# A four-layer graph network kernel: the attention scores of layers 1 and 3 are made transposed, and norms, masks and memory places change with them

## The chip, the core and the metric

The kernel runs on one core of a Trainium2 chip. A core has several engines that each work through their own queue in order: PE (TensorE, matrix products and transposes into the accumulation memory PSUM), DVE (VectorE), ACT (ScalarE), POOL (GpSimd) and SP (SyncE, which here issues the DMAs). PSUM is used as banks of 128 partitions by 512 float32 numbers. The metric is the time of one execution on the device in microseconds.

## What is computed

The input x holds 32 batches of 512 nodes with 128 features each; adj is one 512 x 512 matrix of zeros and ones for all of them. Everything is float32. Four graph layers follow one another, each as `x = layernorm(x + layer(x))`. The batches don't depend on each other.

- Layer 0: scores `e[i,j] = x[i]·a_i + x[j]·a_j`, normalised over the whole 512 x 512 matrix, multiplied by adj, leaky ReLU (slope 0.2), softmax over i, product with x, sigmoid.
- Layer 1: `h = x Wp + bp`, scores `s_src[i] + s_dst[j]`, leaky ReLU, masked by adj, softmax over j, product with h, layer norm and ReLU (gives h_gat); then `(1+eps) h_gat + A h_gat`, a matrix W1, layer norm, ReLU, a matrix W2, and ReLU of the sum with h_gat.
- Layer 2: two matrices, mixed by a constant 512 x 512 attention matrix that depends on adj only.
- Layer 3: as the first half of layer 1, with other weights and with self loops in the mask; softmax, product with h, then ELU.

The core of layers 1 and 3 is, in the reference's words:

```python
e = leaky_relu(e_src[:, :, None] + e_dst[:, None, :], 0.2)
e = where(adj == 0, -1e9, e)
attn = softmax(e, axis=-1)
h_prime = einsum('bij,bjo->bio', attn, h)
```

## The kernel before

A batch is held as four tiles of 128 nodes (NB = 4), a 512 x 512 score matrix as four tiles of 128 x 512. The setup (`prepare_l1`, `prepare_l2`, `prepare_l3`, lines 598 to 771) makes the masks, the transposed matrices and the constants once. Then each batch goes through `statistics0` (line 889), `layer0` (956), `layer1` (981), `layer2` (1042) and `layer3` (1067).

The functions don't emit instructions at once. A recorder (`Recorder`, line 281) writes down every operation with what it reads and writes, for all 32 batches; every operation is emitted at line 432, which is why the profile shows that one line. `Recorder.order` (line 349) then replays an order kept in the text `ORDER`: each byte chooses one of the operations whose inputs are ready. On the way it gives every tile a place: SBUF buffers (BUFFERS = 70), small buffers (SMALLS = 110), PSUM banks (BANKS = 8). In gaps that its own cost list foresees on PE it puts filler transposes, named warm (`fill`, line 395). Each engine then runs its queue strictly in this order, with some ten batches in flight at a time.

The parts that the change touches, by tile name as the profile prints it:

- Layer 0: DVE forms `e_r = (p_s_r + tb) * adj_t` out of PSUM, ACT applies Prelu and then Exp with a sum.
- Layers 1 and 3 (`masked_softmax`, line 863): the row of s_dst is spread over all partitions, by four transposes into PSUM (p_d_g, p_d_a) or, for layer 3 of batches 5 to 29, by DMA through a line in memory (turnedd_a, lined_a, d_a). DVE adds the mask to it and takes each row's maximum in one instruction (`e_g`, `e_a`); ACT applies Prelu (with s_src as bias) and Exp (with the maximum as bias, and a sum read out). Rows i lie on the partitions.
- The product with h needs j on the partitions, so PE transposes each e in 16 blocks (p_t_g, p_t_a); DVE copies them out times adj (nm_g), or ACT copies them out (nm_a).
- Layer 1's first norm: mean and variance of p_o_g by DVE (st_go, mv_go), two passes over hg_g by DVE, ReLU by ACT. Its second norm: the same statistics on zz_g, then a scaling by DVE.
- `layer_norm` (line 809): statistics by DVE, the power -0.5 by POOL (rs_r, rs_g, rs_t, rs_a), the scaling by ACT with two pointers (x_r, x_g, x_t, x_a).
- Layer 3's end: Relu, Exp and a third step on ex_a by ACT, then DVE.

POOL has the powers, three 128 x 512 products a batch (xs_r, hb_g, xbias_t) and set-up work.

Of the kernel before, what the change touches and what calls it, by code (L numbers as in the profile page):

```python
# [17 lines left out]
P = 128  # L18
# [3 lines left out]
FILL = -3.0e38  # L22
# [3 lines left out]
BANKS = 8  # L26
FIRST = 5
FINAL = 6
# [3 lines left out]
ROWS_FROM = 5  # L32
ROWS_LATE = 2
SMALLS = 110
BUFFERS = 70
LINES = 12

ORDER = """
c-mchiH;jFlpNW-@0;vPnz45`2?FH*e=kJ`2!co&*)x*5$;WziutkMgA8{P7cnIh0WXEw3A^uYck<_oahyTIt&yV`CSO0u|pZ8aM&L$~+I2BZ}H?K;cp
Iaa2(Vm0SgR0|s=s_sCQd;L}(@I@55?gI5HmwKgEw@-(iZ!y3Lp!P;ZPYT>=%Wn30&UB+v|6Ke%^a_TjBEY9R$YJB$mcYxmZfH!wM|7v4)woUC-tEIZ^
<T>|Cxyoqzd!DoDYUr@4fTZTWy20-UV-+<yKlRtTe_+!?n>u38fX+(i&qqH=GM$1y@oS?S1eG2k^#g=d9Mo`m9Yh+Td1<mNDz7T+GTTXN7UvNsEJOEtL
++;BJ+*7B4GdwZtoG|IhPWYS1o<fI;pNDvp1(%gQ^eqA@z}UxkxZXkV?6x)>XE(3)$ja~48!mxRmGNm-=Uhf+~u1%*;FNXdj_LSt@%av~TbhvHafE+jj
cRmZ^&jb9If;c&_1AqBN~ho!_t=V<aySbI3jgrwF}WvP&d6^!DOR5R{{FesFxj-a|yaKag3ha@-^<%%fhq|;V%fl{Ix_&8Ub?E2y`7%3*Ay^h-LDRCz;
RxTY@AO^)n5P>JBlMYd%PFMr4g>_gH)Z4k>Ja@_(hxKF<pOuzN&ruVO0|$c&V%2t$a9HE_5-Z`b3K&{Agr|6`vUoG!L&2n^IB-~EQY(p|n2hOksH#+oi
a5tB@zGaQraD5%zg0`_AdwJM4DCZmriUlgQBCzh544FuuLvd%#!(iAx(nuxjWev4l+t;c<Kaj&k*Z+S;k9wp6vqj17!TkgH_S*te-fscKkRN)cPN_vEr
aBE;)+tw0aC2qUMwI0%iuIQOvFqQx}!QO(4>xHq%;z02%`kAV<wgxe>lKEL?KH^T>H+O8<iKHt<2nnphMGMb%`#KrZRqbNf{B87EHGo^t^GoM3b^R4jc
{V2-czy)-uC1#dr^D4sj48G)>&0792=o4h69~pwc;3U5Y47kI4s9g7BjpwXuMM9W;=`=V)9wf@X|LmxU=2OJEGQ1f!77F$WI9A|HlGK=5z^B?9glI^0P  # L50
v3DuG)!YqlF?*^q<MQQOdDmdB?C^CStIFv>SHNY+XuBMrc=m9h;gXKiA383!KTIgj#G{s8FgaNB869DBs3CSy<HH5<(=W%jHaXcVYZ-jwcB=C*_af~J4
fni}LQV@?$;ojn5sWpt}6g){fhmu5)0>o3S5;epEUJ4i;Pa%lSY9OU(G&oM%u1qx=0A13D0p_v>oOLjRrC{1Klo03w1|@(_k{~G_$t;txL{SqObI&Fv3
miumLd+ZM+1n$8unTSo$V%xLZHykBp&i4Yuo%pvmX3LF>!I+3uBWKq6cGgmA#veZVi7FrqgE_ZubIl6I-?|YN(iq257Y)LVbOx1CSn0DVx5-WChuvXz&
iL1izy5N+mm3D17q534TL}tXNoXY0F5z7fD5Pw6&R0-L?^KTHD;d^m@~SPv52S~-|s=Y9uZZ~&Dd-XG>_>Xo#}RY>0xWLsT8iK)<swEixP!sPXrmD6$g
@oS{P?Hryeno=ugpmZ&<{Vn@FNUTzeZsQ>Che+_K8OJ6xdF5gshV>J{Y}Hv*_eV>)e;#+m@o5G)a5NTGyaMT|Kr1?+m6e3UpXmPaQLMUp`s4!|%@m^~<
z#(*ZV*Z{myL>r|D1s=C#gHRwTQfHP@U|7MxY~WR-TzugnK?k5f#wKex!_u(=p~$E$@GY806FPrFt;*(x-9k7x797gpp=&Y(NUT@cJ5`631(R?kf@3To
wKaA{kd6)zIi<Z7`#?|>6MY7hGEdr8E(6ZTqejm_4mhw3LeIdTVtYA7b*!+IDQ(hFwiST^jtMR9i!I=k%Kr&4=uCnnJqqLj<QOuSHE^g%2pOR1w#C6pG
2<v@r8H4v7e*chRwd+?dd-E9m{QCc{)HN_H?bKYlu0Y;=bRb7$Jx*?zg#$DSR;lW(g+zJ#;-Y!8CP^8L0xwzzz_9YYqcfSQfR8Qnjl05sqq4#9JbHc?A
Ck;QRflujwU?IN%<KggRn4{_eepUAcW{k!tAQA0_v2#MBheGM*wobAtRVo0L*XBPf20bS#nxs$Rsl`<zh^j8~j<oWTvi7%GUA#-vpfkrXI51M>n7`A2F
qxQcDgjRW!!nbTh4@mU>*VT#3KA_qUb#?*>(Y*XxVpQyk~x34B=?PKO?b!9Y(ZDRGA6B?&NE4mK-T4+l|gl|5J)K`O3bQi>UiWsVG9f<ymA*3?4Ym<BF  # L60
_S45(7dV;obR4r53h2e_NA$mtcY=NSZTOtT)(8!=k4v9II;d?9$WKQ=AVc;HRRQQ;KBa2a?NSUOxwVa{-VC#}pMwUtnZVIGXt5nJ!=8(sc;jk9OA(R;j
# [59 lines left out]
class Ring:  # L121


    def __init__(self, pool, shape, bufs, name, psum=False):
        self.pool, self.shape, self.name, self.psum = pool, shape, name, psum
        self.slots = [Slot(self, i) for i in range(bufs)]
# [104 lines left out]
def cost(engine, op, args, k):  # L231
# [5 lines left out]
    if engine == "pe":  # L237
        if op == "transpose":
            return 110, 180
        n = args[2].n  # L240
        return (860, 180) if n > 256 else (225, 180)
# [913 lines left out]
```

## Time and profile before

| | |
|---|---|
| median of 3 runs | 1021.2 us (1021.13 to 1022.13) |
| span of the profiled execution | 1019.8 us |
| its time outside the span | not shown by the page; the median is 1.4 us above the span |
| PE, DVE, ACT, POOL busy | 998.3, 968.0, 961.9, 406.4 us |
| most costly groups | products p_o_a, p_o_r, p_o_g: 141.1, 136.2 and 129.2 us of PE |

The span is what passes from the first to the last instruction. "Busy" is the time in which an engine had at least one instruction running, set-up instructions not counted. An instruction's mean duration is longer than its share of the engine when the next one starts before it has ended; the timeline, which lists starts, shows the share.

### The profile page before, as it was taken

How to read it: one execution, taken by the hardware profiler on the slowest of the kernel's cores; microseconds unless marked ns; L12 is line 12 of the kernel's file. 1: busy time of each engine (PE TensorE's matmuls, PEld its weight loads, DVE VectorE, ACT ScalarE, POOL GpSimd, SP SyncE). 2: the span in 40 equal slices, each digit the busy share in tenths (PEclk: the TensorE clock that was granted, in tenths of full speed). 3: DMA queues.
4: the chain of work that ended last, by engine and by line, in shares of the span. 5: the costliest groups of instructions: out<-in, count | busy, mean ns of one | idle time of the engine just before them, and what ended most of it. 6: DMA issues, size and time to landing. Idle time of an engine off the chain costs nothing.

```text
span 1019.8 us, 22710 instructions
## 1 busy us (share of the span) xinstructions
PE 998.3 (98%) x7281; PEld 853.5 (84%) x7281; DVE 968.0 (95%) x4378; ACT 961.9 (94%) x2297; POOL 406.4 (40%) x510
## 2 busy tenths in 40 slices
PE   8999999999999999999999999999999999999994
PEld 7778789879889888888888897888888888779994
DVE  7899999999899999999999999999999998998997
ACT  3597899999999999999999999999999999999997
POOL 7534432352324425343343515342452435244242
PEclk9999999999999999999999999999999999999998
DMA  7000000000110110100111011001001000001003
GB/s 185 28 2 1 1 2 1 2 1 1 32 33 1 36 40 2 42 18 27 33 32 33 22 37 38 22 1 53 12 29 36 11 12 22 23 11 33 12 22 103
DMA packets 42599, 26.81 MB, mean 26 GB/s; under 512 B 4336, under 2 KB 38768, under 8 KB 42480
## 3 DMA queue, kind: packets, MB, share of 16 engines
q1 hardware_dynamic: 42192, 24.84, 8.8%
q8 instruction: 58, 0.95, 0.4%
q14 instruction: 61, 0.50, 0.2%
q10 hardware_dynamic: 288, 0.52, 0.1%
HBM read 16.91 MB, written 8.44 MB: 25 GB/s over the span
## 4 chain that ended last, share of the span: by engine, by line
DVE 39%; ACT 31%; PE 23%; POOL 3%; issue 2%; DMA 1%; POOLq 0%; SPq 0%; DVEq 0%; ACTq 0%
ACT e_a L432 7%; ACT e_g L432 5%; ACT e_r L432 4%; DVE e_g L432 4%; PE p_o_r L432 4%; DVE e_r L432 4%; DVE nm_g L432 3%; PE p_g_g L432 3%; ACT ex_a L432 3%; PE p_o_g L432 3%; DVE e_a L432 3%; DVE zz_g L432 3%; DVE hg_g L432 3%; ACT x_g L432 2%; DVE xa_r L432 2%
## 5 line engine op out<-in xcount | busy, mean ns | idle before, releaser
L432 PE MATMUL p_o_a<-h_a,nm_a 128*128 128x128 f32 x1024 | 141.1, 275 | 0.3 <-ACT nm_a L432 0.3
L432 PE MATMUL p_o_r<-xs_r,e_r 128*128 128x128 f32 x1024 | 136.2, 275 | 0.4 <-POOL xs_r L432 0.3
L432 PEld LDWEIGHTS p_o_a<-h_a,nm_a 128*128 128x128 f32 x1024 | 128.4, 192 | 5.8 <-issue 5.3
L432 PEld LDWEIGHTS p_o_r<-xs_r,e_r 128*128 128x128 f32 x1024 | 125.6, 192 | 4.4 <-issue 3.3
L432 PE MATMUL p_o_g<-h_g,nm_g 128*128 128x128 f32 x1024 | 129.2, 275 | 0.0
L432 PEld LDWEIGHTS p_o_g<-h_g,nm_g 128*128 128x128 f32 x1024 | 122.5, 192 | 4.9 <-issue 4.1
L432 PE MATMUL p_y_t<-l_rest_t,x_g 128*128 128x512 f32 x256 | 120.9, 593 | 0.2 <-ACT x_g L432 0.2
L432 PE MATMUL p_g_g<-a1t,hg_g 128*128 128x512 f32 x256 | 118.7, 595 | 0.7 <-ACT hg_g L432 0.6
L432 ACT ACTIVATE e_a<-e_a,nmx_a 128x512 f32<-128x512 f32 x128 | 92.7, 739 | 2.5 <-DVE nmx_a L432 2.5
L432 ACT ACTIVATE e_r<-e_r,r_r 128x512 f32<-128x512 f32 x128 | 92.6, 728 | 0.4
L432 ACT ACTIVATE e_g<-e_g,nmx_g 128x512 f32<-128x512 f32 x128 | 91.6, 727 | 1.2 <-DVE sh_r L432 0.8
L432 DVE SCALAR_TENSOR_TENSOR e_r<-p_s_r,tb_r,adj_t 128x512 f32<-128x512 f32 x128 | 92.0, 746 | 0.5 <-PE p_s_r L432 0.5
L432 ACT ACTIVATE e_a<-e_a,sd_a 128x512 f32<-128x512 f32 x128 | 89.8, 740 | 0.0
L432 ACT ACTIVATE e_g<-e_g,sd_g 128x512 f32<-128x512 f32 x128 | 86.7, 730 | 0.6 <-DVE mx_g L432 0.3
L432 DVE TENSOR_TENSOR nm_g<-p_t_g,adj_t 128x512 f32<-128x512 f32 x128 | 82.9, 684 | 0.9 <-PE p_t_g L432 0.8
L432 PE MATMUL p_t_a<-ident,e_a 128*128 128x128 f32 x512 | 82.2, 273 | 0.8 <-ACT e_a L432 0.7
L432 DVE CUSTOM_DVE_ANT_0 e_g<-p_d_g,mask 128x512 f32<-128x512 f32 x128 | 82.2, 688 | 0.6 <-PE p_d_g L432 0.5
L432 ACT ACTIVATE e_r<-e_r 128x512 f32<-128x512 f32 x128 | 77.8, 636 | 5.0 <-DVE e_r L432 4.6
L432 PEld LDWEIGHTS p_g_g<-a1t,hg_g 128*128 128x128 f32 x256 | 44.7, 190 | 39.4 <-issue 35.3
L432 PE MATMUL p_t_g<-ident,e_g 128*128 128x128 f32 x512 | 73.0, 273 | 0.2 <-DVE sh_r L432 0.2
L432 POOL TENSOR_TENSOR hb_g<-hg_g,b_bc 128x512 f32<-128x512 f32 x32 | 41.7, 1303 | 68.2 <-ACT hg_g L432 67.9
L432 PEld LDWEIGHTS p_y_t<-l_rest_t,x_g 128*128 128x128 f32 x256 | 43.6, 191 | 30.1 <-issue 27.3
(211 smaller groups left out, 2902.3 us busy)
## 6 DMA issues: line engine op xcount, KB each, us to landing
x_in<-in_x SPq DMA_DIRECT2D x32, 256.0 KB
out<-x_a SPq DMA_DIRECT2D x32, 256.0 KB
d_a<-lined_a SPq DMA_DIRECT2D x25, 256.0 KB
lined_a<-turnedd_a SPq DMA_DIRECT2D x100, 0.5 KB
adj_n<-in_adj ACTq DMA_DIRECT2D x2, 256.0 KB
adj_n<-in_adj SPq DMA_DIRECT2D x2, 256.0 KB
w<-in_L_gnn_W SPq DMA_DIRECT2D x3, 64.0 KB
a_ij<-in_L_gnn_a SPq DMA_DIRECT2D x1, 128.0 KB
```

The lines of the kernel that those rows point to most:

```text
L432: f(*[real(a) for a in args], **{n: real(a) for n, a in k.items()})
```

## The change

Leaky ReLU can be written as `0.2 t + 0.8 max(t, 0)`, and with `t = s[i] + d[j]` the part `0.2 s[i]` cancels in the softmax over j, so that `exp(0.8 (max(d[j], -s[i]) - top[i]) + 0.2 d[j])` is left, where top[i] is the row's maximum of d with the mask, times 1.25 (and the mask with it). This is computed with j on the partitions from the start:

- `score_rows` takes the row maximum (top) as before, from p_d_g or p_d_a, into a PSUM corner and without using the tile that it writes; makes `bend` on DVE, spreads it over the partitions by four transposes (p_g_g, p_g_a), and spreads top by DMA (turnedm, linem, m_g, m_a) for every batch of both layers.
- Layer 1: DVE forms `max(p_g_g, d[j]) - m_g` in a PSUM bank (p_e_g), ACT applies Exp in place, DVE multiplies by adj_t (nm_g). Layer 3: DVE forms `max(p_g_a, d[j]) + mask3_t` (e_a), POOL subtracts m_a, ACT applies Exp. The transposes of e, nm_a and both Prelus are gone.
- h gets a 129th column that gives the row sums out of the product (`products`); ACT writes h_g with a bias instead of DVE. Products have 129 columns, features 131. The weights are centred over features at set-up, so that means vanish.
- Layer 1's norms: ACT squares with a sum instead of DVE's statistics; hg_g by a product with gat_g in PSUM and one pass with max; the second scaling by ACT (zs_g).
- x_g and x_t are scaled without being shifted (`scaled`); x_r and x_a keep the shift.
- Layer 0: ACT applies Prelu out of PSUM with tb as bias, POOL multiplies by adj_t, ACT applies Exp.
- Layer 3's end: one Exp by ACT, a product and minimum by POOL, then DVE in PSUM.
- One PSUM bank ("own") is taken out of the ring for operands of DVE: a_ij, top, some statistics. BANKS = 7, BUFFERS = 57, eight buffers of their own for h, SMALLS = 120.
- A new ORDER text; some entries of the cost list differ.

The diff, cut to its core (set-up, cost list and the order text left out):

```diff
-BANKS = 8
+BANKS = 7
-BUFFERS = 70
+BUFFERS = 57
+FEATS = 8
...
+    feats = Ring(big, [P, NB * HW], FEATS, "feat")
+    own = V(Tl(Ring(ps, [P, 512], 1, "own", True, True), "own"))
...
+    a_ij = own[:, 0 : 2 * D].rearrange("p (k d) -> p k d", k=2)
+    R.dve.tensor_copy(a_ij, a_both)
...
+    def scaled(dst, y, r):
+        for c in range(NB):
+            R.act.activation(dst[:, c, :], y[:, c, :], AF.Identity, scale=r[:, c : c + 1])
+    def normalised(dst, y, more, name, b, by_act=True):
+        mv = corner([P, NB, 2], "mv" + name, b)
+        statistics(y, mv)
+        ve = small([P, NB], "ve" + name)
+        R.dve.tensor_scalar(ve, mv[:, :, 1], LN_EPS, None, ALU.add)
+        r = power(ve, name)
+        mr = corner([P, NB], "mr" + name, b)
+        R.dve.tensor_tensor(mr, mv[:, :, 0], r, ALU.mult)
+        shift = small([P, NB], "sh" + name)
+        R.dve.tensor_scalar(shift, mr, -1.0, more, ALU.mult, ALU.add)
...
+    def features(xt, wx, more, name):
+        h = V(Tl(feats, "h" + name)).rearrange("p (c d) -> p c d", c=NB)
+        for k in range(0, NB, 2):
+            p = bank("h" + name)[:, 0 : 2 * HW].rearrange("p (c d) -> p c d", c=2)
+            for c in range(2):
+                R.pe.matmul(p[:, c, :], xt[:, blk(k + c)], wx, start=True, stop=True)
+            R.act.activation(h[:, k : k + 2, :], p, AF.Copy, bias=more)
+        return h
...
+    def score_rows(h, mask, name, b):
+        pd = rows_of(h[:, :, DST], "d" + name)
+        top = corner([P, NB], "top" + name, b)
+        for c in range(NB):
+            R.dve.tensor_tensor_reduce(
+                buffer("any" + name), pd, mask[:, c, :], 1.25, LOWEST, ALU.add, ALU.max, top[:, c : c + 1]
+            )
+        bend = small([P, NB], "bend" + name)
+        R.dve.scalar_tensor_tensor(bend, top, 0.8, h[:, :, SRC], ALU.mult, ALU.min)
+        top_row = rows_by_dma(top, "m" + name)
+        low = small([P, NB], "low" + name)
+        R.act.activation(low, h[:, :, DST], AF.Copy, scale=LEAKY)
+        return rows_of(bend, "g" + name), top_row, low
...
     def layer0(xb, s, r, tb, b):
-            R.dve.scalar_tensor_tensor(t, p_s, tb[:, j : j + 1], adj_t[:, j, :], ALU.add, ALU.mult)
-            R.act.activation(t, t, AF.Prelu, alpha=LEAKY)
+            if by_pool(b, j):
+                R.act.activation(t, p_s, AF.Prelu, bias=tb[:, j : j + 1], alpha=LEAKY)
+                R.pool.tensor_tensor(t, t, adj_t[:, j, :], ALU.mult)
...
     def layer1(xb, b):
+        h = features(xt, C["l1_wx"], 0.0, "_g")
+        pg, top, low = score_rows(h, C["mask1"], "_g", b)
-        e, z = masked_softmax(sd, C["mask1"], "_g", False)
         for j in range(NB):
-            pt = bank("t_g")
-            for c in range(NB):
-                R.pe.transpose(pt[:, blk(c)], e[c][:, blk(j)], ident)
-            R.dve.tensor_tensor(nm[j], pt, adj_t[:, j, :], ALU.mult)
+            e = bank("e_g")
+            R.dve.scalar_tensor_tensor(e, pg, h[:, j, DST : DST + 1], top, ALU.max, ALU.subtract)
+            R.act.activation(e, e, AF.Exp, bias=low[:, j : j + 1], scale=0.8)
+            R.dve.scalar_tensor_tensor(nm[j], e, 1.0, adj_t[:, j, :], ALU.min, ALU.mult)
+        po = products(nm, h, "_g")
...
+                R.act.activation(
+                    buffer("any_go")[:, 0:D], p[:, c, 0:D], AF.Square, accum_out=sq[:, 2 * k + c : 2 * k + c + 1]
+                )
...
+            R.dve.tensor_tensor(
+                p[:, :, 0:D], p[:, :, 0:D], C["gat_g"].unsqueeze(1).to_broadcast([P, 2, D]), ALU.mult
+            )
+                R.dve.scalar_tensor_tensor(
+                    hg[:, 2 * k + c, :], p[:, c, 0:D], r[:, 2 * k + c : 2 * k + c + 1], C["gat_nb"], ALU.mult, ALU.max
+                )
...
+            R.act.activation(buffer("any_gz")[:, 0:D], zz[:, c, :], AF.Square, accum_out=sq[:, c : c + 1])
+        scaled(zs, zz, power(ve, "_gz"))
...
     def layer3(xb, b):
+        for j in range(NB):
+            R.dve.scalar_tensor_tensor(
+                e[j], pg, h[:, j, DST : DST + 1], C["mask3_t"][:, j, :], ALU.max, ALU.add
+            )
+            R.pool.tensor_tensor(e[j], e[j], top, ALU.subtract)
+            R.act.activation(e[j], e[j], AF.Exp, bias=low[:, j : j + 1], scale=0.8)
+        po = products(e, h, "_a")
...
+            R.act.activation(ex[:, c, :], po[c // 2][:, c % 2, 0:D], AF.Exp, scale=rz[:, c : c + 1])
+        R.pool.tensor_scalar(ex, ex, math.exp(-1.0), 1.0, ALU.mult, ALU.min)
```

## The prediction

> **What bounds the kernel now.** First the page's first two parts and the windows: is one engine short of time, or are they all?
>
> ```profile
> PE 998.3 (98%) x7281; PEld 853.5 (84%) x7281; DVE 968.0 (95%) x4378; ACT 961.9 (94%) x2297; POOL 406.4 (40%) x510
> POOL 7534432352324425343343515342452435244242
> PEclk9999999999999999999999999999999999999998
> ...
> 500.00:600.00 100.00, 99.54 (x749) 86.72 (x748) 99.18 (x453) 100.00 (x242) 36.69 (x46) 1.00 0.09 25
> 1000.00:1020.00 20.00, 6.93 (x58) 6.28 (x56) 12.75 (x59) 12.95 (x37) 6.35 (x10) 0.81 0.42 119
> ```
>
> PE, DVE and ACT are all full; only POOL has room. The granted clock is full. The chain that ended last confirms it: it hops over all three, and no line of code carries more than 7%.
>
> ```profile
> DVE 39%; ACT 31%; PE 23%; POOL 3%; issue 2%; DMA 1%; POOLq 0%; SPq 0%; DVEq 0%; ACTq 0%
> ```
>
> So the forecast is a sum for each engine, and the largest decides. A busy PE may hide gaps, so next the timeline: does the next matmul start where the last one's share ends?
>
> ```profile
> 209.91 0.60 PE L432 MATMUL p_t_a<-ident,x_t 128*128 128x128 f32 x4
> 210.34 1.88 PE L432 MATMUL p_y_t<-l_rest_t,x_g 128*128 128x512 f32 x4
> 212.06 0.38 PE L432 MATMUL p_o_r<-xs_r,e_r 128*128 128x128 f32 x2
> ...
> 250.40 3.73 PE L432 MATMUL p_o_g<-h_g,nm_g 128*128 128x128 f32 x32
> 253.97 1.88 PE L432 MATMUL p_y_t<-l_rest_t,x_g 128*128 128x512 f32 x4
> ```
>
> From start to start (a matmul is two records, a transpose one): a 128-column matmul 3.57/16 = 0.223 us, a 512-column one 1.72/2 = 0.86, a transpose 0.43/4 = 0.11. Counted out: 2387 x 0.223 + 288 x 0.86 + 1983 x 0.11 = 998, the busy time of the page. PE is packed; its 21.5 us of idle lie at the ends (12.2 after the last matmul, 1.5 at the start, 2.9 in one wait).
>
> For DVE and ACT I take pitches too, start to start in the timeline of 300 to 700, since an instruction's mean overlaps its successor. DVE: 128x512 with a pointer 0.655 (e_r), without 0.60 (nm_g), maximum 0.61, 128x128 with pointer 0.26, 128x256 0.34, statistics 0.195 + 0.08, four-column steps 0.07. ACT: 128x512 with a pointer 0.61, Prelu without 0.52, copy from PSUM 0.47, sum read-out 0.10; 128x128 with two pointers from SBUF 0.39, with one from PSUM 0.25.
>
> **The change part by part.** Counts are from the instruction order of both programs; 32 batches.
>
> PE. The 1024 transposes of e_g and e_a go. New are the rows of bend (256 transposes) and 100 more of p_d_a, which came by DMA; 16 for mask3_t; 58 fewer warm fillers: -710 x 0.11 = -78.1. Five or six small set-up matmuls: +1.3. Products of 129 columns instead of 128, features of 131 instead of 130: p_h_a x4 (two matmuls of 130) takes 0.45, so at most +2.3. Sum 998.3 - 74.5 = 924.
>
> DVE, per batch. Gone: e_r 4 x 0.655; nm_g from p_t_g 4 x 0.60; zz scaling 4 x 0.29; the second pass over hg 4 x 0.26; h_g 2 x 0.34; the statistics of o_g and z_g 8 x 0.275; small steps (sd, nmx, ve_go, two shifts, tb) and late copies 1.4: together 11.5. New: p_e_g 4 x 0.655; nm_g from p_e_g 4 x 0.60; e_a 4 x 0.655; the gat_g product 2 x 0.34; small steps (bend, mr, ve, the second dev, halves of y_a, turned, reciprocals) 0.75: together 9.1. Net -2.4 x 32 = -77, +4 of set-up (weight means, a_ij to PSUM, b1): 895.
>
> ACT, per batch. Two of three Prelus go (4 x 0.61 each) and the third now has a pointer (+0.2); the sums of e_g and e_a 8 x 0.10; nm_a copies 1.7; the whole-tile steps on ex_a and hg_g's Relu 1.5; x_g and x_t lose the bias pointer, 8 x 0.1. New: squares of o_g and z_g 8 x 0.25, scaling of z_g 4 x 0.25, h_g 0.5, squares of the sum column and low 0.5. Net about -5.5 x 32 = -176, +5 set-up: 791.
>
> POOL. Two more 128x512 products in every j: 256 of them. Nearest rows:
>
> ```profile
> L432 POOL TENSOR_TENSOR hb_g<-hg_g,b_bc 128x512 f32<-128x512 f32 x32 | 41.7, 1303 | 68.2 <-ACT hg_g L432 67.9
> L432 POOL TENSOR_TENSOR xs_r<-x_in,rz_r 128x512 f32<-128x512 f32 x32 | 33.7, 1053 | 57.6 <-DVE rz_r L432 23.7 <-issue 7.8 <-PE p_o_t L432 6.2
> ```
>
> 256 x 1.30 = 333 (1.05 would give 269; I take hb_g, which reads two full tiles as the new ones do). With ex_a 18, ve_go 9, tb 9, less ve_r and ve_a 17: about 758. POOL stays under PE, with some 20% left. What waits on it: xs_r, five powers a batch and xbias queue behind the products, so each may come one or two products (1.3 to 2.6 us) later; 11 batches are in flight in both orders (products of layer 0 ahead of those of layer 3), so I cost this at nothing in the middle.
>
> [...]
>
> Does a fuller POOL stall DVE? The trace shows when it does:
>
> ```profile
> 506.37 1.17 DVE L432 TENSOR_SCALAR zz_g<-zz_g,mv_gz,rs_gz 128x128 f32<-128x128 f32 x1
> 506.41 1.04 POOL L432 TENSOR_TENSOR xs_r<-x_in,rz_r 128x512 f32<-128x512 f32 x1 [2.50 <-DVE var_r L432]
> ```
>
> 0.33 us of work took 1.17 until POOL's product was done: all operands in SBUF. The maximum over p_d_g (one operand in PSUM) takes 0.690 alone and 0.687 beside POOL. In the new program every large DVE step has a PSUM operand or is a statistic (st_a: 0.282 and 0.275), but for the last three batches' x_a; so I add nothing.
>
> DVE writing to PSUM has no row: 12 large and some 20 small such writes a batch. Reading PSUM costs DVE nothing (y_t from p_o_t 685 ns, y_a from SBUF 684). The largest effect of place in the trace is ACT's, 0.05 us (a whole tile takes 0.47 when read from PSUM by xt_g's copy, 0.52 when read from SBUF by hg_g's Relu). So per write between -0.05 and +0.05: DVE 895 - 51 to 895 + 51. I take 0, DVE's own row, and keep both ends. [...]
>
> DMA and SP. Every layer 1 and 3 now gets its maximum by DMA: 64 rows instead of 25.
>
> ```profile
> 453.85 2.07 SPq L432 DMA_DIRECT2D lined_a<-turnedd_a  x4
> 457.08 0.33 SPq L432 DMA_DIRECT2D d_a<-lined_a  x1
> ```
>
> SP is held 3.6 us a row, 230 us in all with the wait for the line, and the row is there at most 7.4 us after turning (3.6, and the first 256 KB of adj_n landed within 3.83). Behind such a wait on SP stand x_in and out, both early or free in the middle. 39 more broadcasts of 256 KB are 10 MB on queues that are under 10% busy. Layer 3 waits for its row on POOL, whose other products queue behind; layer 1 on DVE at p_e_g, and a late row there stops all batches' DVE steps, then ACT and PE. While 11 batches are in flight 7 us are covered: nothing; in the last ones the cover is gone.
>
> Ends. Before the first p_o_r POOL now has four products more, 5.2 us, and PE has set-up matmuls to fill them with: between 0 and 5, I take +2. At the end POOL has 20 products (26 us) for the last five batches while PE needs 80 x 0.223 = 18 us for their products, and the rows' 7 us: between 0 and 10, I take +4. The steps after the last matmul are the same in number (12 us).
>
> Sum: 924 + 21.5 + 2 + 4 = 951.5 of span. Around the span lie 1.4 us (median 1021.2 less 1019.8; the page has no time of the profiled execution itself): **953 us**, -6.7%.
>
> **The rivals.** *DVE becomes the bound*, by writes to PSUM or by steps that wait in its order for POOL (nm_g for the Exp, hg_g for rs_go, y_a for ex_a). For: 895 is only 29 under PE, and in the old kernel DVE had 52 us of idle with PE as its bound. Against: PSUM reads are free. At 0.05 us a write DVE has 946, and with the old ends 967 to 1000.
>
> *PSUM banks run out: slower.* There are 7 instead of 8 for tiles, and a tile stays longer: e_g (DVE, ACT, DVE) 2.1 us x 4, o_g through squares, power and hg_g 7.4 x 2, o_a 5.5 x 2, z_g 6.3; all tiles of a batch sum to about 91 us by pitches (before: 58). 91 x 32 / 7 = 416 us at least. It decides once holding stretches to 1020/416 = 2.45 times these. In the old trace p_d_g is held 3.84 us (median) where pitches give 3.1, p_h_g 2.26 where they give 1.07: 1.2 to 2.1 times. At 2.6 the span would be 1082. For it: short tiles stretch most. Against: most of the sum is in long ones.
>
> *Little gain because the removed work was beside other work*: can't be all, since all three full engines lose 74 to 180 us; if POOL's queue or the row's latency costs PE 1.5 us a batch, 1000.
>
> **How the numbers follow.** PE stays the bound: 0.66, 941 to 965 (924 plus 16 of ends that can't go, to 924 plus 41). DVE or waits: 0.22, 965 to 1000. Between 1000 and the old time: 0.04. Slower by banks: 0.07; unchanged 0.01. 0.2% is what a measurement tells here. Faster 0.92. 940 to 995 leaves out some 0.03 below and 0.15 above (0.03 of the DVE case, and all beyond 1000).
>
> **What would show it.** Right: p_t_g and p_t_a from e gone, PE busy near 924 and 99 of 100 us in the middle windows, DVE near 895, ACT near 790, POOL near 760; POOL products at 1.3 us; DVE's p_e_g at e_r's 746 ns. Wrong: PE with gaps in the middle, released by nm_g or e_a (DVE or POOL late) or by a reader of a PSUM tile (banks); DVE writes to PSUM longer than rows that write SBUF; POOL over 90%.

## The result and the profile after

The changed kernel takes 1063.8 us (median of 4 runs, 1063.6 to 1064.6), the kernel before 1021.2 in the same session: 1.0418 times as long, 95% interval 1.0403 to 1.0433. It is slower by 4.2%; the forecast was 953 us, 6.7% faster. The profiled execution has a span of 1062.9 us.

First the busy times of the page of the changed kernel, and its slices for the granted clock:

```profile
PE 965.6 (91%) x6583; PEld 794.6 (75%) x6583; DVE 954.7 (90%) x3635; ACT 816.0 (77%) x2399; POOL 770.0 (72%) x819
...
PEclk9989999999999999999999999999999999999996
```

The work moved as the change says: PE has 698 instructions fewer, ACT lost 146 us, POOL gained 364. That POOL's 770.0 is near the 758 of the forecast is luck: ex_a alone came to 42 us more than was put down, other rows to some 30 less. But DVE has 954.7 where I expected 895, and no engine is full: a program with four engines at 91, 90, 77 and 72% waits for itself. The clock is granted but for the ends.

The stretches of the same two programs show where. Columns are the window, its length, the busy time of PE, PEld, DVE, ACT and POOL, then the granted clock, the DMA share and GB/s. Kernel before, first 100 us and last 120:

```profile
0.00:100.00 100.00, 94.25 (x655) 80.02 (x656) 88.06 (x348) 68.01 (x151) 51.92 (x69) 0.98 0.22 55
900.00:1019.80 119.80, 106.93 (x824) 94.90 (x823) 105.50 (x456) 112.84 (x289) 43.59 (x61) 0.97 0.13 39
```

Changed kernel, the same ends, and the window from 500 to 600 that the prediction showed:

```profile
0.00:100.00 100.00, 80.22 (x600) 74.79 (x601) 83.00 (x435) 78.20 (x188) 82.40 (x107) 0.93 0.28 71
500.00:600.00 100.00, 93.90 (x631) 74.67 (x630) 95.51 (x377) 79.25 (x241) 74.88 (x79) 1.00 0.14 41
943.00:1062.90 119.90, 92.86 (x624) 77.81 (x622) 98.27 (x372) 74.44 (x212) 89.11 (x82) 0.90 0.14 38
```

PE lost 14 us of work in the first 100 and 14 in the last 120, and in the middle it is no longer full; DVE is the fullest there. The timeline of PE has holes that the old one hadn't; here one of 1.05 us, which DVE's y_a ended:

```profile
412.49 1.05 PE L434 MATMUL p_o_r<-xs_r,e_r 128*128 128x128 f32 x8
414.59 0.71 PE L434 MATMUL p_h_a<-l_wx,xt_a 128*128 128x131 f32 x4 [1.05 <-DVE y_a L434]
```

What is dear is in the groups (busy time and mean of one, then idle time before them; an aggregate is the step that makes a mean and a variance out of six numbers). POOL and DVE of the changed kernel:

```profile
L434 POOL TENSOR_TENSOR e_a<-e_a,m_a 128x512 f32<-128x512 f32 x128 | 161.4, 1279 | 18.7 <-DVE e_a L434 9.4 <-DMA m_a<-linem_a 7.2 <-DVE rz_a L434 1.0
L434 POOL TENSOR_SCALAR ex_a<-ex_a 128x512 f32<-128x512 f32 x32 | 61.8, 1933 | 12.5 <-ACT ex_a L434 10.8
...
L434 DVE BATCH_NORM_AGGREGATE own<-st 128x2 f32<-128x6 f32 x256 | 47.3, 185 | 5.4
L434 DVE DVE_READ_ACCUMULATOR2_ANT own<- 128x1 f32 x256 | 36.3, 142 | 0.0
L434 DVE DVE_READ_ACCUMULATOR2_ANT n_r<- 128x1 f32 x216 | 17.9, 83 | 0.0
L434 DVE BATCH_NORM_AGGREGATE mv_g<-st 128x2 f32<-128x6 f32 x128 | 14.6, 159 | 0.0
```

Two rows of the kernel before stand against them, POOL's step on ex_a (a multiply and an add there, in the three batches where POOL had it) and the read-out of a maximum into SBUF:

```profile
L432 POOL TENSOR_SCALAR ex_a<-ex_a 128x512 f32<-128x512 f32 x3 | 1.9, 621 | 3.3 <-ACT ex_a L432 3.3
...
L432 DVE DVE_READ_ACCUMULATOR2_ANT mx_g<- 128x1 f32 x128 | 11.4, 89 | 0.0
```

Two things stand out. POOL's step on ex_a takes 1933 ns; I had put 18 us for the 29 that are new, which is 0.62 each, the price of the old row. And the same DVE steps are longer where they write the PSUM tile own than where they write SBUF (n_r, mv_g, the old mx_g): the read-out of a sum 142 against 83 and 89 ns. From start to start the difference is larger, in DVE's timeline of the changed kernel:

```profile
403.56 0.30 DVE L434 BATCH_NORM_AGGREGATE mv_t<-st 128x2 f32<-128x6 f32 x3
403.78 0.45 DVE L434 BATCH_NORM_STATS2 st<-y_r 128x6 f32<-128x128 f32 x2
404.15 0.85 DVE L434 BATCH_NORM_AGGREGATE own<-st 128x2 f32<-128x6 f32 x4
404.90 0.15 DVE L434 BATCH_NORM_AGGREGATE mv_g<-st 128x2 f32<-128x6 f32 x1
...
405.61 0.68 DVE L434 CUSTOM_DVE_ANT_0 any_g<-p_d_g,mask 128x512 f32<-128x512 f32 x1
406.21 0.14 DVE L434 DVE_READ_ACCUMULATOR2_ANT own<- 128x1 f32 x1
406.39 0.69 DVE L434 CUSTOM_DVE_ANT_0 any_g<-p_d_g,mask 128x512 f32<-128x512 f32 x1
```

Four aggregates into own take 0.75 us (404.15 to 404.90), 0.19 each; three into mv_t take 0.22, 0.07 each. A maximum with its read-out takes 0.78, where the kernel before had 0.61. And the largest wait of DVE is for POOL's slow step:

```profile
DVE p_o_a L434 <- POOL ex_a L434: 32.9, 28, 2.5
```

The theory after this look: two prices were wrong, ex_a on POOL and small writes to PSUM on DVE, and DVE became the bound. The rivals: waiting in POOL's queue, PSUM banks, the order text itself.

### The profile page after: what moved, and what is told of

Read it like the earlier page. It is cut to its first block, busy times and chain, and to the rows that moved or that the text cites. A ratio compares the mean times of both kernels' runs of the same rounds, so it can differ in the third digit from the quotient of the medians.

```text
span 1062.9 us, 21689 instructions
## 1 busy us (share of the span) xinstructions
PE 965.6 (91%) x6583; PEld 794.6 (75%) x6583; DVE 954.7 (90%) x3635; ACT 816.0 (77%) x2399; POOL 770.0 (72%) x819
## 5 line engine op out<-in xcount | busy, mean ns | idle before, releaser
L434 POOL TENSOR_TENSOR e_a<-e_a,m_a 128x512 f32<-128x512 f32 x128 | 161.4, 1279 | 18.7 <-DVE e_a L434 9.4
L434 POOL TENSOR_TENSOR e_r<-e_r,adj_t 128x512 f32<-128x512 f32 x128 | 160.6, 1278 | 14.1 <-ACT e_r L434 13.6
L434 PE MATMUL p_o_a<-h_a,e_a 128*128 128x129 f32 x1024 | 138.1, 282 | 10.5 <-ACT e_a L434 8.8
L434 PEld LDWEIGHTS p_o_a<-h_a,e_a 128*128 128x128 f32 x1024 | 128.4, 197 | 17.2 <-ACT e_a L434 10.3
L434 PE MATMUL p_o_g<-h_g,nm_g 128*128 128x129 f32 x1024 | 130.3, 276 | 4.5 <-DVE y_a L434 2.1
L434 ACT ACTIVATE e_a<-e_a,low_a 128x512 f32<-128x512 f32 x128 | 91.9, 735 | 26.3 <-POOL e_a L434 25.8
L434 DVE CUSTOM_DVE_ANT_0 any_g<-p_d_g,mask 128x512 f32<-128x512 f32 x128 | 88.2, 689 | 6.4 <-PE p_d_g L434 2.4
L434 DVE SCALAR_TENSOR_TENSOR p_e_g<-p_g_g,h_g,m_g 128x512 f32<-128x512 f32 x128 | 93.6, 749 | 0.2
L434 DVE CUSTOM_DVE_ANT_0 any_a<-p_d_a,mask 128x512 f32<-128x512 f32 x128 | 88.0, 687 | 5.9 <-PE p_d_a L434 1.8
L434 DVE SCALAR_TENSOR_TENSOR e_a<-p_g_a,h_a,mask_t 128x512 f32<-128x512 f32 x128 | 90.5, 740 | 1.8 <-PE p_g_a L434 1.8
L434 POOL TENSOR_SCALAR ex_a<-ex_a 128x512 f32<-128x512 f32 x32 | 61.8, 1933 | 12.5 <-ACT ex_a L434 10.8
```

What stands on the lines that cost most here:

```text
L434: f(*[real(a) for a in args], **{n: real(a) for n, a in k.items()})
```

## Experiments

### The prices by themselves

A kernel of its own runs each step in rows of equal instructions: first seven forms on POOL, 128x512 each (lines 40 to 52), then small and large steps on DVE (66 to 86).

```python
pool.tensor_scalar(g, a, 0.5, 1.0, ALU.mult, ALU.add)    # 40, 8 times
pool.tensor_scalar(g, a, 0.5, 1.0, ALU.mult, ALU.min)    # 42
pool.tensor_scalar(g, a, 1.0, None, ALU.min)             # 44
pool.tensor_scalar(g, a, 0.5, None, ALU.mult)            # 46
pool.tensor_tensor(g, a, b, ALU.mult)                    # 48
pool.tensor_scalar(g, a, 0.5, 0.1, ALU.mult, ALU.max)    # 50
pool.tensor_scalar(g, a, 0.5, 1.0, ALU.add, ALU.mult)    # 52
```

> A kernel of its own that computes nothing of the reference: it runs each disputed step alone, in rows of equal instructions, POOL first and then DVE, so that neither disturbs the other. Theory 1 (prices of two new forms were missed): POOL's 128x512 tensor_scalar takes about 1.9 us whenever a minimum or maximum is one of its operations and 0.62 us for multiply and add; DVE's aggregate of six numbers takes 0.08 us from start to start when it writes SBUF and 0.19 when it writes PSUM, a four-column product 0.07 and 0.14 to 0.18, the sum read-out of a maximum about 0 and 0.12 more; 128x512 steps that write PSUM or SBUF take the same 0.60 to 0.66. Theory 2 (the slowness in the changed kernel comes from other work beside it, such as shared tiles, POOL's or DVE's neighbours): alone, ex_a's form takes 0.62 and the small steps take the same 0.07 to 0.09 into PSUM as into SBUF.

Groups of POOL:

```profile
L42 POOL TENSOR_SCALAR g<-a 128x512 f32<-128x512 f32 x8 | 15.3, 1918 | 0.6
L50 POOL TENSOR_SCALAR g<-a 128x512 f32<-128x512 f32 x8 | 15.3, 1918 | 0.6
L46 POOL TENSOR_SCALAR g<-a 128x512 f32<-128x512 f32 x8 | 11.9, 1488 | 0.6
L44 POOL TENSOR_SCALAR g<-a 128x512 f32<-128x512 f32 x8 | 11.9, 1485 | 0.6
L48 POOL TENSOR_TENSOR g<-a,b 128x512 f32<-128x512 f32 x8 | 10.1, 1262 | 0.5
L52 POOL TENSOR_SCALAR g<-a 128x512 f32<-128x512 f32 x8 | 4.9, 618 | 0.6
L40 POOL TENSOR_SCALAR g<-a 128x512 f32<-128x512 f32 x8 | 4.9, 617 | 4.0 <-DMA a<-in_x 3.4
```

Timeline of DVE, whole rows of the small steps (24 aggregates into SBUF, 24 into PSUM; 16 products of four columns into SBUF, 16 into PSUM, 16 that read PSUM):

```profile
84.36 1.69 DVE L66 BATCH_NORM_AGGREGATE s<-st 128x2 f32<-128x6 f32 x24
85.96 5.33 DVE L68 BATCH_NORM_AGGREGATE p<-st 128x2 f32<-128x6 f32 x24
91.20 1.22 DVE L71 TENSOR_TENSOR s<-s,first 128x4 f32<-128x4 f32 x16
92.34 3.25 DVE L73 TENSOR_TENSOR p<-s,first 128x4 f32<-128x4 f32 x16
95.49 1.19 DVE L75 TENSOR_TENSOR s<-p,first 128x4 f32<-128x4 f32 x16
```

Theory 1 holds for POOL, the aggregates and the products, with nothing beside the steps. With a minimum or a maximum as second operation a step takes three times one that multiplies and adds (1918 ns against 617); what I hadn't expected is that one operation alone (1485 for a minimum, 1488 for a multiplication) is dearer than a multiply-and-add. An aggregate takes 0.067 us from start to start into SBUF and 0.218 into PSUM, a four-column product 0.071 and 0.197; reading PSUM costs nothing (0.068). The large step takes the same into either (8 in 6.25 and in 6.31 us, 0.78 each, which is more than the 0.66 at most that the theory gave; why was not looked for). The sum read-out is not settled by this run: a maximum with its read-out took 0.73 us from start to start into SBUF and 0.79 into PSUM, a difference of 0.06 and not 0.12.

So for these small steps the price of PSUM lies on the destination (0.13 to 0.15 us more) and not on the source (0.068 us from PSUM, 0.071 from SBUF).

### The two prices in the kernel: one, the other, both

```diff
-        R.pool.tensor_scalar(ex, ex, math.exp(-1.0), 1.0, ALU.mult, ALU.min)
+        R.pool.tensor_scalar(ex, ex, math.exp(-1.0), 0.0, ALU.mult, ALU.add)
```

> The changed kernel with one operation of one POOL step altered: ex_a is multiplied by exp(-1) and gets 0 added, in place of the minimum with 1 (so positive values of the last layer are wrong); order, tiles and waits are the same. Theory 1 (ex_a is three times dearer than I put it, and DVE stands behind it in its queue): the step takes 0.62 us, POOL's sum falls by 42 us to about 728, the 33 us that DVE waits for it at p_o_a shrink to under 10, and the time falls by 15 to 35 us, to 1029 to 1049. Rival (DVE has its bound elsewhere and the wait only moves): DVE waits as long for the next late step, and the time falls by less than 8 us.

This kernel leaves the minimum out, so its time is that of less than the whole computation. Measured: 1034.5 us (1.0127 of the kernel before, 1.0110 to 1.0144), 29.3 less than the changed kernel. ex_a took 618 ns, POOL 727.1, and the wait shrank:

```profile
DVE p_o_a L434 <- POOL ex_a L434: 3.6, 6, 1.2
```

Theory 1, in its range: what went is 29.3 us of the 32.9 that DVE had waited; its own sum all but stayed (951.0). Idle time of DVE is time of the kernel here.

Then the small results, in one SBUF tile instead of the PSUM tile:

```diff
+    nook = V(Tl(Ring(big, [P, 256], 1, "nook", True, True), "nook"))
...
-        t = own[:, at : at + n]
+        t = nook[:, at - 2 * D : at - 2 * D + n]
```

> The changed kernel with all the small corners that it keeps in the PSUM tile own (means and variances of two norms, mr, top, and the deviations of layer 0) put into one SBUF tile instead, shared in the same way, with the same order; a_ij stays in PSUM. Theory 1 (small DVE writes to PSUM cost some 0.1 us more each): the aggregates fall from 0.19 to 0.08 us from start to start, DVE's sum falls from 955 to about 890, and since DVE is 95% busy in the middle the time falls by 35 to 60 us, to 1004 to 1029. Theory 2 (the shared tile's waits of DVE on itself are the cost, not the place): the aggregates stay near 0.19, DVE near 955, and the time within 10 us of 1064. Theory 3 (the place in PSUM is what keeps these steps from waiting for POOL): the four-column steps now wait for POOL's products, up to 1.3 us at each of some 6 a batch, and the time rises by 20 us or more.

Measured: 1044.5 us (1.0238, 1.0222 to 1.0253), 19.3 less, and DVE's sum fell by 5 only. The time lies outside all three ranges; theories 1 and 3 are both at work. Start to start, with idle times left out, the 256 read-outs went from about 30 us to under 1 and the 256 aggregates of own from about 45 to 20: some 54 us gained. It is not the read-out's own place alone: the one of dev_r writes SBUF in both programs, and it took 142 ns where the step in front of it wrote eight columns to PSUM and 80 ns here. But steps that now have all tensors in SBUF wait for POOL's products, as a later run with less work on POOL shows (bend_g 437 to 251 ns). Groups of DVE:

```profile
L434 DVE SCALAR_TENSOR_TENSOR bend_a<-nook,h_a 128x4 f32<-128x4 f32 x32 | 15.4, 483 | 0.0
L434 DVE SCALAR_TENSOR_TENSOR bend_g<-nook,h_g 128x4 f32<-128x4 f32 x32 | 14.3, 448 | 0.0
L434 DVE TENSOR_TENSOR nook<-nook,rs_r 128x4 f32<-128x4 f32 x32 | 11.0, 343 | 1.0 <-POOL rs_r L434 1.0
L434 DVE TENSOR_SCALAR sh_r<-nook 128x4 f32<-128x4 f32 x32 | 10.4, 324 | 0.2
```

In the changed kernel these take 143 to 164 ns. The difference in these four rows and the seven like them (ve, dev, sq, sh_a, mr_a) is 55 us. Theory 2, that the shared tile is at fault, falls: the tile is as shared as before and its aggregates take 0.08.

> Both edits together: the minimum left out of ex_a (so positive values of the last layer are wrong) and the small corners in SBUF. Theory 1 (two mis-sized prices are most of the miss): DVE 890, POOL 728, and the time between 965 and 1000, of which up to 25 us are the slower start and the tail. Rival (the order and POOL's queue cost PE as much by themselves): still 1020 or more, with PE idle for waits on POOL and DVE steps that move from one row to the next.

Both edits: 1013.1 us (0.9925, 0.9904 to 0.9946), 50.7 less; the single gains add up to 48.6. That is above the range that theory 1 gave, since DVE's sum stayed at 946 with those waits in it. The short pauses between DVE's instructions (under 0.25 us) fell from 24.9 us in the changed kernel to 4.7, which the busy times don't show.

### An operand in PSUM, but which

> The changed kernel with both prices mended and nothing left out: mv, mr and top lie in an SBUF tile; the four-column steps that read them (bend, ve, mr, shift) take their constant (0.8, 1e-5, 1, -1) as a pointer to a column in PSUM, so that one operand stays there; ex_a becomes 1 - relu(1 - ex/e), a whole-tile Relu on ACT and a multiply-and-add on POOL in place of the minimum. Order as in the changed kernel. Theory 1 (an operand in PSUM, be it only the pointer, keeps a step from waiting for POOL): bend, ve, mr and shift go back to 0.15 us each, DVE's sum falls from 946 in the run with both edits to about 900, and the time from 1013 to between 975 and 1000. Rival (a pointer doesn't count as the operand): these steps stay at 0.25 to 0.48 us, DVE stays near 945 and the time at 1005 to 1020.

```diff
-        R.dve.scalar_tensor_tensor(bend, top, 0.8, h[:, :, SRC], ALU.mult, ALU.min)
+        R.dve.scalar_tensor_tensor(bend, top, c08, h[:, :, SRC], ALU.mult, ALU.min)   # c08: a column in PSUM
```

Measured: 1041.4 us (1.0213, 1.0174 to 1.0252). The rival: a pointer doesn't count. DVE's sum is 960.7, above the 946 of both edits: the rows of bend, ve, mr and shift grew from 84 us to 100. The time is above the rival's range as well; in this version DVE waits 17.1 us for ex_a, behind ACT's Relu and POOL's step. Groups of DVE:

```profile
L434 DVE SCALAR_TENSOR_TENSOR bend_g<-nook,own,h_g 128x4 f32<-128x4 f32 x32 | 15.9, 497 | 0.1
L434 DVE SCALAR_TENSOR_TENSOR bend_a<-nook,own,h_a 128x4 f32<-128x4 f32 x32 | 14.0, 440 | 0.0
```

An output in PSUM doesn't count either, as a later run shows, in which mr reads two SBUF tiles and writes own:

```profile
L434 DVE TENSOR_TENSOR own<-nook,rs_r 128x4 f32<-128x4 f32 x32 | 11.3, 354 | 4.3 <-POOL rs_r L434 3.1
```

That run is the next, with the means alone in SBUF and ex_a without POOL:

> The changed kernel with nothing left out and the same order, mended by what the runs so far taught. Means and variances (mv) of two norms go to SBUF, so the 256 aggregates should take 0.07 us from start to start in place of 0.19 (-30 us of DVE); top, mr and the deviations stay in PSUM, so bend, mr and shift keep an operand there and don't wait for POOL. ve is added on POOL just before the power (64 x 0.3 = 19 us of POOL, -5 of DVE). ex_a is made on ACT alone as Exp(-Relu(1 - p rz)), with the negated rz copied by ACT, and has no POOL step (POOL -62, ACT about +25). Theory (DVE's sum is the bound, and the time is that sum plus some 66 us of start, tail and single waits, as in the three runs without the wait for ex_a: 1013 against 946, 993 against 926, 1039 against 973): DVE about 918, the time 975 to 995, faster than the kernel before. Rival (the wait for ex_a and POOL's place in the chain give way to waits for ACT, which gets the work): DVE near 920 but p_o_a waits 20 us or more for ACT's ex_a, and the time is 1000 to 1025.

```diff
-        R.dve.tensor_scalar(ve, mv[:, :, 1], LN_EPS, None, ALU.add)
+        R.pool.tensor_scalar(ve, mv[:, :, 1], LN_EPS, None, ALU.add)     # beside the power
...
-            R.act.activation(ex[:, c, :], po[..], AF.Exp, scale=rz[:, c : c + 1])
-        R.pool.tensor_scalar(ex, ex, math.exp(-1.0), 1.0, ALU.mult, ALU.min)
+            R.act.activation(ex[:, c, :], po[..], AF.Relu, bias=1.0, scale=minus_rz[:, c : c + 1])
+        R.act.activation(ex, ex, AF.Exp, scale=-1.0)
```

Measured: 1033.0 us (1.0110, 1.0093 to 1.0127). DVE had 938, not 918: the aggregates' row fell by 19 us and ve's 9.8 us were gone, but mr's two rows grew from 10.6 to 21.7. The wait for ex_a was gone (4.7 us at p_o_a), so the rival as I had put it is not what happened, though its range came nearer. Nor does the sum plus 66 us hold: the time lies 95 us above DVE's sum. DVE waited 21.9 us for ACT (9.5 with both edits), and its pauses under 0.25 us came to 19.7 (4.7 with both edits), for the read-outs still write PSUM.

With two tensors from SBUF the four-column steps bend and mr took 238 to 497 ns in the runs so far, whether their pointer or their output lay in PSUM, and 143 to 166 with one of the two from PSUM in the changed kernel. Two tensors aren't needed for it: sh_r and ve_r have a single one, and took 324 and 314 ns with it in SBUF where they had taken 153 and 152 with it in PSUM.

### POOL's queue and the banks

Both runs change the kernel with both edits (1013 us).

> The kernel of both edits (minimum left out, corners in SBUF; 1013 us) with POOL relieved besides: layer 0's product with adj_t is replaced by a multiply and add with constants (so layer 0's mask is left out), 0.62 us in place of 1.28. POOL's sum falls by 128 x 0.66 = 84 to about 644. Theory A (POOL's queue, in which powers and xs_r stand behind products, holds the other engines up: the term that the forecast put at nothing): the time falls by more than DVE's own sum does, by 20 to 45 us, to 968 to 993. Theory B (DVE's own work is the bound in the middle and POOL's queue is covered): the time falls only by what DVE's sum loses in waits for POOL, 5 to 15 us.

```diff
-                R.pool.tensor_tensor(t, t, adj_t[:, j, :], ALU.mult)
+                R.pool.tensor_scalar(t, t, 0.5, 0.0, ALU.mult, ALU.add)
```

Measured: 993.4 us (0.9736, 0.9720 to 0.9752), 19.7 less. The pages of the kernel of both edits and of this one:

```profile
PE 945.3 (93%) x6583; PEld 787.8 (78%) x6583; DVE 946.3 (94%) x3635; ACT 810.4 (80%) x2399; POOL 727.9 (72%) x819
...
PE 937.9 (95%) x6583; PEld 783.9 (79%) x6583; DVE 926.2 (93%) x3635; ACT 808.0 (82%) x2399; POOL 645.8 (65%) x819
```

DVE's sum fell by 20.1, since its all-SBUF steps waited less (bend_g 437 to 251 ns): what these steps wait for is POOL. Theory B in its sense, time following DVE's sum; the fall itself lies above B's 5 to 15 and just under A's 20 to 45. With 82 us less on POOL no time was won beyond DVE's.

> The kernel of both edits (minimum left out, corners in SBUF; 1013 us) with an eighth PSUM bank: a_ij moves to SBUF as well, so that the bank of the tile own joins the seven, with the same order. The 216 steps xa_r then have all operands in SBUF, which may cost DVE up to 20 us in waits for POOL; their rows will show it. Theory A (seven banks hold PE up, the rival of the forecast): the time, less what xa_r's rows gained, falls by 15 us or more. Theory B (banks are not short): the time stays within 5 us of 1013 plus what xa_r's rows gained.

```diff
-BANKS = 7
+BANKS = 8
...
-    own = V(Tl(Ring(ps, [P, 512], 1, "own", True, True), "own"))
+    own = V(Tl(Ring(big, [P, 256], 1, "own", True, True), "own"))
```

Measured: 1039.0 us (1.0173, 1.0149 to 1.0197), 25.9 more. xa_r's row grew by 27.2 (50.3 to 77.5). Theory B: once xa_r's 27.2 are taken off, the eighth bank saved about 1 us, in this kernel and this order.

```profile
L434 DVE CUSTOM_DVE_ANT_0 xa_r<-x_in,own 128x128 f32<-128x128 f32 x216 | 77.5, 402 | 0.1
```

In these three runs (both edits, POOL relieved, eight banks) the time is DVE's sum plus 66 or 67 us: DVE is the bound in them.

### All small steps mended

Means and top in SBUF; the source column copied into PSUM by ACT, so that bend has one tensor there; ve, mr and shift on POOL, ex_a on ACT. The diff shows the new steps in short form; in the run they are issued at the places of the ones they replace, so that the order stays.

```diff
             R.act.activation(h[:, k : k + 2, :], p, AF.Copy, bias=more)
+            R.act.activation(src[:, k : k + 2], p[:, :, SRC], AF.Copy, bias=more)      # src: in own
...
-        R.dve.scalar_tensor_tensor(bend, top, 0.8, h[:, :, SRC], ALU.mult, ALU.min)
+        R.dve.scalar_tensor_tensor(bend, top, 0.8, src, ALU.mult, ALU.min)
...
-        R.dve.tensor_tensor(mr, mv[:, :, 0], r, ALU.mult)
-        R.dve.tensor_scalar(shift, mr, -1.0, more, ALU.mult, ALU.add)
+        R.pool.tensor_tensor(mr, mv[:, :, 0], r, ALU.mult)
+        R.pool.tensor_scalar(shift, mr, -1.0, more, ALU.mult, ALU.add)
```

> The changed kernel with nothing left out and the same order, with every small step of DVE either kept from writing PSUM or taken off DVE. mv and top go to SBUF (aggregates and sum read-outs: -24 and -30 us by the start-to-start sums of the two programs). bend reads its second tensor, a copy of the source column, out of PSUM, where ACT puts it with two more short copies a layer (about 128 x 0.2 = 26 us of ACT), so that bend shouldn't wait for POOL. ve, mr and shift run on POOL beside the power (POOL +50 or so, DVE -18). ex_a by ACT as in the run before. Theory (the forecast's DVE sum of 895 was right but for the price of small writes to PSUM; without them DVE falls to about 875 to 890 and PE with 924 of work is the bound that I put down): the time is 955 to 985. Rival (the order, made for other prices, keeps DVE or PE waiting some 90 us in any case, as in the last run, where DVE had 938 and the time was 1033): 985 or more, with the DVE sum under 895.

Measured: 1009.2 us (0.9883, 0.9865 to 0.9901), 1.2% less than the kernel before. The steps cost what the theory said (timeline of DVE):

```profile
410.64 0.68 DVE L434 CUSTOM_DVE_ANT_0 any_g<-p_d_g,mask 128x512 f32<-128x512 f32 x1
411.25 0.08 DVE L434 DVE_READ_ACCUMULATOR2_ANT nook<- 128x1 f32 x1
411.25 0.69 DVE L434 CUSTOM_DVE_ANT_0 any_g<-p_d_g,mask 128x512 f32<-128x512 f32 x1
```

A maximum takes 0.61 from start to start again. DVE's sum is 890.5, but the rival had the time right: no engine is full, and DVE stands idle for 117 us, 51 more than with both edits. Most of this is waiting for ACT, which the mending gave 37 us of work: DVE waits 43.3 us for it against 9.5, and 14.4 for POOL's power rs_go against 3.3. The mended steps, ex_a among them, explain 54.6 of the 111 us between forecast and result, not all of it. Stretches of this kernel:

```profile
0.00:100.00 100.00, 79.60 (x616) 73.79 (x617) 78.08 (x422) 80.45 (x202) 88.32 (x126) 0.98 0.28 71
300.00:700.00 400.00, 389.97 (x2790) 326.78 (x2790) 380.07 (x1472) 361.06 (x1144) 301.12 (x392) 1.00 0.13 38
887.00:1007.10 120.10, 98.21 (x683) 81.94 (x682) 94.61 (x356) 91.33 (x287) 82.94 (x110) 0.96 0.15 45
```

The middle is nearly full on PE; most of what is left lies at the start and at the end.

### Is it POOL that makes the start late?

> The mended kernel of the last run (nothing left out, 1009 us, the order of the changed kernel) with layer 0's product with adj_t put back on DVE for batches 1 to 4 and 28 to 31, with Prelu after it, at the same places in the order; the 24 batches between keep it on POOL. POOL loses 8 x 4 x 1.28 = 41 us, half of it in the first 150 us, DVE gains 32 x 0.66 = 21. Theory (POOL is the bound of the first 100 us, where it was 88% busy and PE 80%, against 52% and 94% in the kernel before; the forecast allowed 2 us for it): POOL is busy under 75 of the first 100 us, PE over 85, and the time falls by 6 to 15 us, to 994 to 1003. Rival (the order sets the start, not POOL): less than 4 us of change.

```diff
-                R.act.activation(t, p_s, AF.Prelu, bias=tb[:, j : j + 1], alpha=LEAKY)
-                R.pool.tensor_tensor(t, t, adj_t[:, j, :], ALU.mult)
+                R.dve.scalar_tensor_tensor(t, p_s, tb[:, j : j + 1], adj_t[:, j, :], ALU.add, ALU.mult)
+                R.act.activation(t, t, AF.Prelu, alpha=LEAKY)
```

Measured: 1029.3 us (1.0075, 1.0060 to 1.0090), 20 more. POOL went from 88 to 57 of the first 100 us, and PE did no more than before:

```profile
0.00:100.00 100.00, 78.45 (x548) 73.53 (x549) 79.24 (x410) 68.37 (x168) 56.58 (x92) 0.88 0.27 68
```

Both the theory and the size that the rival gave fall. In an order made for POOL's product, the DVE step stands where ACT's Prelu stood, and ACT waits for it (15.0 us at e_r); that this makes what stands behind it in both queues late fits the 20 us but was not tested by itself, and the granted clock of the stretch is lower too (0.88 against 0.98). A cleaner answer lies in the run with POOL relieved, where no step changed its place: there POOL had 65.3 of the first 100 us instead of 84.1, and PE 83.0 instead of 80.9. POOL's work is a small part of the late start.

### A new order

The order text of the changed kernel comes with a function of prices (`cost`), which puts ex_a's step on POOL at 190 + 0.77 x 512 = 584 ns and doesn't ask where a small result goes; how the text itself was made, the kernel doesn't show. Two runs have an order made anew with the measured prices: always the most urgent ready step on the engine that is free first, with the urgency of each kind of step and each batch found by a search over these prices. So they differ from the old order by the prices and by the way of making it, and what they gain can't be divided between the two. First with the mended steps:

> The mended kernel of 1009 us with the same work on the same engines, the small results that it moved now recorded as operations of their own, and a new order text, made with the prices that these runs measured (ex_a without POOL, aggregates and read-outs into SBUF at 0.07 and 0, powers at 1.0, products at 1.25, short ACT copies at 0.06 to 0.3). The order of the changed kernel was made with the prices of its function cost, which gives POOL's step on ex_a 190 + 0.77 x 512 = 584 ns and a small write to PSUM the same as one to SBUF. Theory (of the 56 us between 1009 and the forecast's 953 a good part is an order that was made for other prices: engines wait for steps that the order thought done): the time falls by 15 to 40 us, to 970 to 995, with PE over 96% busy between 300 and 700 us. Rival (start, tail and queue waits of this program can't be ordered away): 1000 or more.

Measured: 987.5 us (0.9669, 0.9653 to 0.9685). This version is 3.3% faster than the kernel before. Its page and stretches:

```profile
PE 948.7 (96%) x6775; PEld 800.5 (81%) x6775; DVE 893.0 (91%) x3443; ACT 840.4 (85%) x2623; POOL 746.8 (76%) x979
```

```profile
0.00:100.00 100.00, 80.04 (x615) 74.05 (x616) 73.43 (x344) 77.78 (x202) 87.46 (x123) 0.96 0.23 60
300.00:700.00 400.00, 398.87 (x2884) 338.89 (x2883) 390.23 (x1560) 371.60 (x1186) 325.46 (x426) 1.00 0.14 40
863.40:983.40 120.00, 107.02 (x797) 91.73 (x795) 96.36 (x350) 80.22 (x250) 72.41 (x94) 0.97 0.12 34
```

PE is full in the middle (398.87 of 400) and the tail is as good as in the kernel before (107.0 of 120 against 106.9); the start stays 14 us poorer. Then the changed kernel itself, with nothing mended:

> The changed kernel itself, with nothing mended (POOL's minimum on ex_a at 1.92 us, aggregates and read-outs into PSUM) and nothing left out; only the order text is new, made in the same way as that of the last run, with the measured prices. It fills the fourth corner of a square: 1064 us (dear steps, old order), 1009 (mended, old order), 987 (mended, new order). Theory A (the dear steps cost DVE's time as such; the order is worth the same 22 us with and without them): 1030 to 1050, DVE's sum near 955. Theory B (an order that knows the prices can put other work where DVE waited, for ex_a and at the ends, so that DVE's sum of 955 and some 40 us of ends are all that is left): 995 to 1015. Theory C (the order has no part in it without the mending): above 1055.

Measured: 1029.9 us (1.0076, 1.0059 to 1.0093), at the lower edge of theory A's range (1030); the order is worth more than its 22 us. DVE's sum is what A said:

```profile
PE 960.2 (93%) x6689; PEld 799.8 (78%) x6689; DVE 954.3 (93%) x3635; ACT 813.3 (79%) x2399; POOL 768.9 (75%) x819
```

The four corners:

| | order of the change | new order |
|---|---|---|
| steps of the change | 1063.8 | 1029.9 |
| steps mended | 1009.2 | 987.5 |

Mending is worth 54.6 us in the one order and 42.4 in the other, a new order 33.9 and 21.7. In the first row DVE keeps 954 us of work; what the new order takes away is waiting (DVE's pauses of over 0.25 us between its first and last instruction fall from 75.2 to 40.8 us).

## Why the prediction was wrong

- **DVE writing to PSUM, "I take 0".** This term failed, and its bounds of 0.05 us did too. They came from where a whole 128x512 tile lies, and for such tiles 0 was right (6.25 and 6.31 us for eight). The writes that cost are those of one to eight columns: 0.13 to 0.15 us more alone for aggregates and products, and in the kernel about 30 us for 256 read-outs and 24 for 256 aggregates. I had 12 large and 20 small writes a batch in one term with one price.
- **"ex_a 18" on POOL.** The row measured 61.8, 59.9 more than before, because I gave a step with a minimum the price of the multiply-and-add in the old row (621 ns). That is 42 us on an engine with room; they cost 29.3 us of time, because DVE stands in line for the result. I had named this wait, "y_a for ex_a", in a rival and not in the sum.
- **DVE's sum, 895.** With the small writes gone it is 890.5 in the mended kernel, where ve, mr and shift have moved to POOL; with these at 0.07 each it would be about 13 higher. The count was good to 2%; the price of place was missing.
- **PE's sum, 924, and PE as the bound.** Right, but reached only after mending and reordering: the 948.7 us there hold 219 fillers where the order of the change has 27; without those 192 x 0.11 = 21 it is 927.6, and PE is full between 300 and 700. In slower versions the same PE instructions show a longer busy time (6583 of them: 965.6 in the changed kernel, 937.9 at 993 us), which a sum of pitches taken from a packed stretch doesn't hold. ACT's sum, 791, measured 816.0; ACT wasn't the bound, and the difference was not looked into.
- **"I cost this at nothing in the middle" (POOL's queue).** Right as far as it was tested, in a version that DVE bounds: with 82 us less on POOL the time fell only as DVE's sum did. In the mended kernel with the old order DVE waits 14.4 us for POOL's rs_go, so it isn't nothing in every version.
- **The order.** The forecast had no term for it. I read from the order text what stands before what and took the distances to be covered. Another order of the same work was worth 22 to 34 us. That the old one loses this because it was made for other prices is argued, not shown: the old way of ordering was not run with the new prices.
- **Ends.** Start: +2 put down, 12 to 15 us less work of PE in the first 100 us measured, with the steps of the change or mended and in both orders. I had counted the four products ahead of the first p_o_r; POOL makes 35 of them in these 100 us of the changed kernel (42.9 us), for the nine batches that start there. That unloading POOL gains only some 2 us of PE's work there was shown; whether another set-up would help was not tried. Tail: +4 put down, 14 less work of PE measured in the last 120 us, 8 with the new order alone, none with the mended steps and the new order.
- **DMA rows "covered: nothing".** Right: POOL's product waits 7.2 us in all for its row. **POOL doesn't stall DVE where an operand lies in PSUM.** Right for a tensor that is read from PSUM (the maximum over p_d_g took 688 ns in the kernel before and 689 in the changed kernel, with 364 us more work on POOL), and the run with the corners in SBUF shows the price of the contrary, 55 us.
- **The rivals.** The first, DVE as the bound through PSUM writes and waits for POOL, is what happened, at 1064 instead of 967 to 1000: its price per write was too low, and it had no term for the order. A slower kernel had a chance of 0.07, all of it through PSUM banks, so the direction was missed by the same terms. PSUM banks are refuted for the order at hand (about 1 us for an eighth one).
- **The 256 products on POOL.** They took 1279 ns (e_a) and 1278 (e_r), as the row of hb_g said (1303). DVE's nm_g, a product of the same size, took 684 ns in the kernel before; at its pitch of 0.60 the 256 would have added an estimated 154 us to DVE, 895 + 154 = 1049, which no run has tried. That they weren't the cause of the miss is only in part shown: making 128 of them cheaper won no time but what DVE's all-SBUF steps waited, steps whose operands the changed kernel reads from PSUM, and putting those of eight batches back on DVE cost 20 us, in an order that wasn't made for it.

The miss of 111 us as a sum, with the edits taken in this sequence: ex_a 29, the other mended steps 25, the order 22 (after mending), and 34.5 between 953 and the 987.5 of the best version: 21 of fillers (which the order puts where it foresees PE waiting), 7 of idle time beyond the 27.5 that I had allowed, 3.6 of PE's sum, and 2.7 between the profiled execution's span and the median.

## What to carry to other kernels

Here a price belonged to a form: engine, both operations, size and place of the result (one operation changed, 617 to 1918 ns on POOL; one place changed, 0.067 to 0.218 us on DVE). Where a change brings a form that no row shows, bound it by rows of its own size and its own operations, or measure it alone before building on it; and ask of each slow form on an engine with room who stands in its queue for the result. When prices change or a step changes engines, try a fixed order made anew: here it brought 22 us after a mending that had brought 55.

## What was not expected of the hardware

- POOL, 128x512, SBUF: multiply-and-add 0.617 us, a multiplication or a minimum alone 1.49, with a minimum or maximum as second operation 1.92.
- DVE results of a few columns: 0.067 us (aggregate) and 0.071 (product) from start to start into SBUF, 0.218 and 0.197 into PSUM; a whole 128x512 tile takes the same into both (0.78, 0.79), and reading four columns from PSUM is free (0.068).
- DVE's four-column steps with two SBUF tensors waited for POOL (bend_g 437 ns, and 251 with 82 us less work on POOL), and took about as long where their pointer or their output lay in PSUM (bend 440 and 497 ns, mr 354, against 143 to 166 with one of the tensors in PSUM).
